# Second routed layer of a graph and mixture-of-experts network: how its experts' rows are weighted, fetched and summed

## The chip, the cores and the metric

The kernel runs on one core of a Trainium2 chip, as one program of 261270 instructions. The metric is the device time in microseconds (us); the time before is the median of three runs. A profiled execution, recorded by the hardware profiler, stands beside them with its own time and span. The engines are called PE (matrix multiplies, with PEld its weight loads), DVE, ACT and POOL (element work), SP (DMA issue); POOL and ACT issue DMAs too.

## The reference

Eight layers follow each other over 625 nodes of 512 features, each adding to x. The layer that the change touches is the fourth, a mixture of experts in two levels: 4 groups of 8 experts, of which each node takes 2 groups and in each group 2 experts.

```python
def _L1_ffn_ref(inp, ln_g, ln_b, wg_group, wg_inner, W1, b1, W2, b2, gln_g, gln_b):
    x = inp.reshape(-1, d)
    gw = _topk_gate(x @ wg_group, GK, G)              # GK = EK = 2, G = 4, E = 8
    z = _layernorm(x, ln_g, ln_b)
    out = jnp.zeros_like(x)
    for g in range(G):
        iw = _topk_gate(z @ wg_inner[g], EK, E)
        moe = jnp.zeros_like(z)
        for e in range(E):
            h = jax.nn.relu(z @ W1[g, e] + b1[g, e])
            moe = moe + iw[:, e:e + 1] * (h @ W2[g, e] + b2[g, e])
        y = _layernorm(z + moe, gln_g[g], gln_b[g])
        out = out + gw[:, g:g + 1] * y
    return out.reshape(b, t, d) + inp
```

The layer before it is a graph convolution (L1_gnn), the one behind it a routed graph convolution (L2_gnn), and behind that comes a recurrent layer (L2_ffn) which fills most of the span.

## The kernel before

The 625 nodes lie as five tiles (t = 0 to 4) of P = 125 rows. The kernel is written layer by layer; when it is built, a scheduler puts the instructions of each engine into one fixed order and sets the semaphores, so neighbouring layers and stages may mix. `tc.issue_after(i)` makes what its block issues on i's engine stand behind i in that order.

L1_ffn in stages. **Front**: the small weights (wg, wi, ln_g, ln_b, rb, gb) are loaded from ACT's queue (L1105, L1108, L106 in row_bcast, L1143 to L1145); x, normed, becomes xin (L153), z is its layer norm (L174, L175) and is written to the DRAM table `nodes`; both are transposed (L183) and copied by ACT (L186). **Routing**: gate logits on PE (L285), the best two per group, and from them, for each of the 4 choices (c) of a node, its expert, its rank within the expert (`rk`) and its score. `at` (L1219) is a one-hot matrix of ranks, `named` (L1207) one of experts weighted with the node's number; their product pw (L1220) summed gives `who`: which node sits in which of the 128 places (SLOTS) of each of the 32 experts (ALL). `to` gives, for each choice of each node, the row of the DRAM table `made` in which its result will be. A branch (L1276) calls L1_late where more than 128 nodes chose one expert; in these data it is not taken.

**Experts**: fetch(e) gathers an expert's 128 rows from `nodes` on POOL (L1154), ten experts ahead. places (transposes, L1307, copy xg L1310), first (eight PE passes, L1320, and a relu on ACT to hid, L1322) and second (one PE product y, L1328, an ACT copy ys, L1330, a 256 KB write to `made` from SP, L1331) run for experts 0 to 31. In iterations 2 to 16 inputs() puts in, one at a time, what doesn't depend on the experts: for each tile the bias sums (L1297, added to z by L1298 into zb[0] and zb[1], one for each of a node's two groups, j) and x + xin (POOL, L1293) with the gain's bias (L1292, L1294).

**Sum and norm**: take(j) gathers from `made` on POOL (L1340), two rows for each node and tile, into buffers r0 and r1, which j = 0 and j = 1 share. norm(j, ts) adds them to zb[j] times their scores (DVE, L1351), takes statistics (L1352, L1353), the root through ACT (L127 in rsqrt, with DVE's L128 to L132), and applies gain and weight (L1362 on PE, L1363, L1364 on DVE) to x. take(0) stands behind expert 24's work, as every j = 0 choice lies in groups 0 to 2; take(1) behind the last expert. C.seen takes the statistics of the finished x (L144 to L146), from which L2_gnn norms it (L153); that layer loads its adjacency counts m_count (L222, from SP), casts them (L191, L193), multiplies the gate (L285) and the counts (L237) and begins its expert products (L292).

Of the kernel before, what the change touches and what calls it, by code (L numbers as in the profile page):

```python
# [30 lines left out]
KC = D // 128  # L31
# [687 lines left out]
def L0_ffn(C):  # L719
# [11 lines left out]
    with ExitStack() as st:  # L731
# [24 lines left out]
        with ExitStack() as st2:  # L756
# [32 lines left out]

            C.made1 = C.dram.tile([4 * N + 32 * SLOTS, D], F32, name="made1")  # L790
            for r in range(0, 4 * N, 128):
                n = min(128, 4 * N - r)
                nc.sync.dma_start(C.made1[r:r + n], zero[:n])
# [244 lines left out]
def L1_gnn(C):  # L1038

    nc, tc, I = C.nc, C.tc, C.ins  # L1040
    with ExitStack() as st:
        E = st.enter_context
        pool = E(tc.tile_pool(name="b", bufs=1))
        ps = E(tc.tile_pool(name="b_ps", bufs=2, space=PSUM))
        bias = C.row_bcast(pool, I["L1_gnn_b"], D, "bias")
        m = C.load_graph(pool, "weighted")
        xn = pool.tile([P, NT, D], F32, name="xn")
        C.normed(xn)
        xT = pool.tile([128, KC, N], F32, name="xT")
        C.feature_major(ps, xT, xn)  # L1050
        w = C.w_next
        h = pool.tile([P, NT, D], F32, name="h")
        for t in range(NT):
            ph = ps.tile([P, D], F32, name="ph")
            C.linear(ph, xT, t, w)
            C.copy(t, h[:, t], ph)
        for t in range(NT):
            po = ps.tile([P, D], F32, name="ph")
            C.aggregate(po, m, t, h)
            y = pool.tile([P, D], F32, name="y", bufs=2)  # L1060
            nc.vector.tensor_add(y, po, bias[:P])
            nc.vector.scalar_tensor_tensor(y, y, 0.0, xn[:, t], op0=ALU.max, op1=ALU.add)
            nc.vector.tensor_add(C.x[:, t], C.x[:, t], y)
            C.seen(t)
    C.ahead.close()


def L1_ffn(C):
# [11 lines left out]
    with ExitStack() as st:  # L1080
# [20 lines left out]

        DENSE = G * N
        made = C.made1
        wg = pool.tile([128, KC, G], F32, name="wg")
        nc.scalar.dma_start(wg, W("wg_group").rearrange("(k p) g -> p k g", p=128))  # L1105
        wi = pool.tile([128, KC, G, EX], F32, name="wi")
        for g in range(G):
            nc.scalar.dma_start(wi[:, :, g], W("wg_inner")[g].rearrange("(k p) e -> p k e", p=128))  # L1108

        C.gate_w = C.small.tile([128, KC, 4], F32, name="gate_w", bufs=1)  # L1110
# [3 lines left out]
        z = pool.tile([P, NT, D], F32, name="z")  # L1114
        C.layernorm(z, xin, C.row_bcast(pool, W("ln_g"), D, "ln_g"), C.row_bcast(pool, W("ln_b"), D, "ln_b"))
        C.by_parts(nodes.rearrange("(t p) d -> p t d", p=P), z)
# [21 lines left out]

        rb, gb = R([128, D], "rb"), R([128, D], "gb")
        nc.gpsimd.memset(rb, 0.0)  # L1140
        nc.gpsimd.memset(gb, 0.0)
        for j in range(2):
            nc.scalar.dma_start(rb[32 * j:32 * j + 32], W("b2").rearrange("g e d -> (g e) d"))  # L1143
            nc.scalar.dma_start(rb[64 + 32 * j:64 + 32 * j + G], W("gln_g"))
        nc.scalar.dma_start(gb[64 + G:64 + 2 * G], W("gln_b"))  # L1145
        who_f, who = R([SLOTS, ALL], "who_f"), pool.tile([SLOTS, ALL], U32, name="who")
# [5 lines left out]
        def fetch(e):  # L1152
            fetched[e] = at_pool.tile([SLOTS, D], F32, name="at_e")
            nc.gpsimd.indirect_dma_start(out=fetched[e], out_offset=None, in_=nodes[:, :],  # L1154
                                         in_offset=bass.IndirectOffsetOnAxis(ap=who[:, e:e + 1], axis=0))

        with tc.tile_pool(name="c_ps", bufs=2, space=PSUM) as ps, tc.tile_pool(name="c_x", bufs=1) as xpool:
# [66 lines left out]
            for e in range(AT):  # L1224
                fetch(e)
            top = R([1, 1], "top")
# [17 lines left out]
            for i in range(2):  # L1244
                pick(score[:, 2 * i:2 * i + 2], ss_g[:, :, :G, i])
            pick(wj, gate[:, :, :G])
            nc.vector.tensor_tensor(tmp, OH, score[:, :, :, None].to_broadcast(wide4), ALU.mult)
# [17 lines left out]
            nc.vector.tensor_mul(beyond, beyond, lj)  # L1265
            nc.vector.tensor_add(slot[:, :2], slot[:, :2], beyond)
            nc.vector.tensor_mul(late[:, 2:], slot[:, 2:], lj)
            nc.vector.tensor_sub(slot[:, 2:], slot[:, 2:], late[:, 2:])
            nc.vector.tensor_copy(to, slot)
            nc.vector.tensor_tensor(score[:, :2], score[:, :2], lj, ALU.max)  # L1270
            nc.vector.tensor_mul(late[:, 2:], score[:, 2:], lj)
            nc.vector.tensor_sub(score[:, 2:], score[:, 2:], late[:, 2:])

# [50 lines left out]
        def second(e):  # L1324
# [4 lines left out]
            ys = work.tile([128, D], F32, name="ys", bufs=4)  # L1329
            nc.scalar.copy(ys[:SLOTS], y[:SLOTS])  # L1330
            nc.sync.dma_start(made[DENSE + e * SLOTS:DENSE + (e + 1) * SLOTS], ys[:SLOTS])  # L1331

        rows = {}

        def take(j):
            rows[j] = [work.tile([P, NT, D], F32, name=f"r{i}", bufs=1) for i in range(2)]
            upto = DENSE + (ALL - EX * (1 - j)) * SLOTS
            for t in range(NT):
                for i in range(2):
                    nc.gpsimd.indirect_dma_start(out=rows[j][i][:, t], out_offset=None, in_=made[:upto, :],  # L1340
                                                 in_offset=bass.IndirectOffsetOnAxis(ap=to[:, 2 * i + j, t:t + 1], axis=0))

        def norm(j, ts):
# [5 lines left out]
            for t in ts:  # L1349
                for i in range(2):  # L1350
                    nc.vector.scalar_tensor_tensor(moe[:, t], rows[j][i][:, t], score[:, 2 * i + j, t:t + 1], moe[:, t], op0=ALU.mult, op1=ALU.add)  # L1351
                nc.vector.bn_stats(st_[:, t], moe[:, t])  # L1352
                nc.vector.bn_aggr(mv[:, t], st_[:, t])  # L1353
# [13 lines left out]
        for e in range(ALL + 1):  # L1367
# [4 lines left out]
            if e:  # L1372
                second(e - 1)
            if 2 <= e < 17:
# [1025 lines left out]
```

## Time and profile before

| what | us |
|---|---|
| median of 3 runs (lowest, highest) | 4655.87 (4653.85, 4656.43) |
| the profiled execution | 4661.62 |
| its span (mean granted clock of PE 0.960) | 4659.8 |
| L1_ffn, from its first load to the last x (L1364) | 749.8 to 944.9 |
| `who` ready | 796.8 |
| first expert's transposes | 805.7 |
| take(0)'s ten issues | 886.0 to 900.7 |
| take(1)'s ten issues | 910.8 to 926.7 |
| first L292 of the next layer | 977.65 |

The engines' busy time in stretches of the layer (x counts instructions; PEclk is the granted clock of PE, 1 being full speed; DMA share is that of the 16 DMA engines; the last column is GB/s):

```profile
core 0: us, PE busy (x) PEld busy (x) DVE busy (x) ACT busy (x) POOL busy (x), PEclk, DMA share, GB/s
753.00:763.00 10.00, 0.02 (x1) 0.03 (x1) 8.47 (x23) 0.86 (x3) 5.74 (x5) 0.50 1.02 276
763.00:774.00 11.00, 11.00 (x83) 10.53 (x83) 7.25 (x37) 6.20 (x10) 0.00 (x0) 0.81 1.03 369
...
815.00:895.00 80.00, 80.00 (x434) 53.50 (x433) 24.16 (x36) 32.41 (x66) 25.12 (x25) 1.00 0.87 298
895.00:903.00 8.00, 0.93 (x9) 0.73 (x7) 4.91 (x11) 0.33 (x2) 4.77 (x4) 0.83 0.79 231
903.00:912.00 9.00, 8.10 (x12) 2.41 (x12) 8.50 (x27) 2.41 (x7) 1.19 (x1) 0.69 0.29 109
912.00:963.00 51.00, 24.42 (x74) 15.86 (x75) 37.49 (x113) 7.69 (x17) 11.97 (x10) 0.50 0.33 88
```

A row is read from left to right: in 815 to 895 PE is busy all 80 us at full clock; in 895 to 903 it has 0.93 us of work.

### The profile page before, as it was taken

To read this page: it belongs to the slowest core of one execution; us is meant where nothing else is said; L and a number is where in the kernel's file an instruction comes from. 1 tells how busy PE (TensorE), PEld (TensorE's weight loads), DVE (VectorE), ACT (ScalarE), POOL (GpSimd) and SP (SyncE) were. 2 spreads that over 40 slices of the span, in tenths; PEclk is the share of its full clock that TensorE was granted. 3 is DMA by queue.
4 is the path that set the end of the run, shared out by engine and by line. 5 is a ranking of instruction groups with operands and counts; after the bars stand their busy time and mean duration, and the time that the engine had idled before them with its cause. 6 is when DMAs were issued, how large, how long until landed. Compare 5 with 4: busy or idle time off the path is not lost. (4 is left out here: it accounts for less than half of the span.)

```text
span 4659.8 us, 261270 instructions
## 1 busy us (share of the span) xinstructions
PE 4305.1 (92%) x110568; PEld 3367.1 (72%) x110568; DVE 2735.3 (59%) x13565; ACT 1373.1 (29%) x5465; POOL 275.6 (6%) x777
## 2 busy tenths in 40 slices
PE   8998997889999799999999999999999999998888
PEld 6666764566566678888888888887888888887555
DVE  7535016431166566677667677766676777676358
ACT  8533111311156222222222222222222222222146
POOL 0000001300000000000000000000000000000001
PEclk9997997889999899999999999999999999999888
DMA  1131983711166222222222222221000000000200
GB/s 43 43 140 37 323 281 102 250 49 50 63 215 237 59 42 45 44 47 49 43 47 49 44 52 49 45 45 39 8 8 8 7 7 9 7 9 10 87 10 12
DMA packets 487820, 315.92 MB, mean 68 GB/s; under 512 B 287531, under 2 KB 386599, under 8 KB 486461
## 3 DMA queue, kind: packets, MB, share of 16 engines
q1 hardware_dynamic: 469706, 289.62, 22.5%
q0 software_dynamic: 8800, 16.92, 1.3%
q10 hardware_dynamic: 9092, 6.87, 0.6%
q8 instruction: 84, 1.38, 0.1%
q14 instruction: 138, 1.13, 0.1%
HBM read 261.52 MB, written 51.77 MB: 67 GB/s over the span
## 5 line engine op out<-in xcount | busy, mean ns | idle before, releaser
L2015 PE MATMUL pa<-wp,left 128*23 128x256 bf16 x32080 | 1011.2, 274 | 0.0
L2015 PEld LDWEIGHTS pa<-wp,left 128*23 128x23 bf16 x32080 | 816.3, 94 | 65.8 <-issue 4.4
L2015 PE MATMUL pb<-wp,left 128*23 128x128 bf16 x30000 | 541.3, 220 | 0.6
L2015 PEld LDWEIGHTS pb<-wp,left 128*23 128x23 bf16 x30000 | 491.5, 94 | 7.0 <-issue 2.5
L2103 ACT ACTIVATE seq<-ga 128x8 f32<-128x8 f32 x625 | 131.7, 211 | 1179.1 <-DVE ga L2161 1179.1
L2159 DVE STREAM_TRANSPOSE col<-pa 128x256 f32<-128x256 f32 x625 | 281.6, 451 | 303.7 <-PE pa L2015 303.4
L2003 PEld LDWEIGHTS pb<-wsel,cs 128*4 128x4 f32 x5000 | 151.0, 83 | 262.1 <-DVE cs L2170 241.0
L2073 PE MATMUL acc<-xslot,wslot 128*128 128x160 f32 x1250 | 337.7, 352 | 0.0
L2003 PE MATMUL pb<-wsel,cs 128*4 128x8 f32 x5000 | 217.1, 169 | 112.2 <-DVE cs L2170 45.3
L2030 PE MATMUL po<-o,left 128*23 128x128 f32 x5416 | 285.7, 281 | 13.4 <-issue 12.5
L2027 PE MATMUL po<-w,left 128*23 128x128 bf16 x14912 | 293.3, 219 | 0.0
L1991 POOL TENSOR_TENSOR seq<-seq,cs 128x4 f32<-128x4 f32 x625 | 126.3, 202 | 2648.7 <-ACT seq L2103 2648.7
L2096 ACT COPY xrow<-xlb 1x4 f32<-1x4 f32 x625 | 122.5, 196 | 540.4 <-ACTq L2094 540.4
L2153 DVE COPY col<-gxb 128x16 f32 x625 | 114.3, 183 | 219.0 <-issue 219.0
L2008 PE MATMUL pb<-wsel,left 128*4 128x8 f32 x5000 | 217.6, 170 | 25.6
L2073 PEld LDWEIGHTS acc<-xslot,wslot 128*128 128x128 f32 x1250 | 186.6, 189 | 67.7 <-issue 0.2
L2027 PEld LDWEIGHTS po<-w,left 128*23 128x23 bf16 x14912 | 234.7, 94 | 0.0
L2027 PE MATMUL po<-o_rest,left 128*23 128x128 bf16 x7588 | 220.5, 220 | 1.9 <-DMA o_rest<-parts_o 1.9
L2008 PEld LDWEIGHTS pb<-wsel,left 128*4 128x4 f32 x5000 | 150.3, 83 | 84.4 <-DVE left L2134 71.7
L2134 DVE TENSOR_TENSOR left<-th,so 128x4 f32<-128x4 f32 x625 | 104.2, 167 | 179.4 <-ACT so L2109 179.4
L2163 DVE STREAM_TRANSPOSE col<-pb 128x128 f32<-128x128 f32 x625 | 197.9, 317 | 6.0 <-PE pb L2015 4.8
L2168 DVE STREAM_TRANSPOSE col<-po 128x128 f32<-128x128 f32 x625 | 198.4, 317 | 2.8 <-PE po L2027 2.8
(555 smaller groups left out, 7119.2 us busy)
## 6 DMA issues: line engine op xcount, KB each, us to landing
ring<-in_L_ffn_W_dram SPq DMA_DIRECT2D x80, 1024.0 KB
xslot<-xTd SPq DMA_DIRECT2D x384, 80.0 KB
wslot<-in_L_ffn_WihT_dram SPq DMA_DIRECT2D x384, 64.0 KB
gxb<-gx SPq DMA_DIRECT2D x124, 160.0 KB
w<-in_L_ffn_WihT_dram SPq DMA_DIRECT2D x16, 1024.0 KB
raw<-in_L_ffn_WhhT_dram SPq DMA_DIRECT2D x28, 512.0 KB
made<-ys SPq DMA_DIRECT2D x39, 256.0 KB
w<-in_L_gnn_Wl_dram SPq DMA_DIRECT2D x8, 1024.0 KB
```

The source lines that it names most:

```text
L1991: pool.tensor_tensor(seq[:, 2, 1::2], seq[:, 1, 1::2], cell_c, ALU.mult).then_inc(sem["ifg"])
L2003: pe.matmul(lg, cs[:, 2 * s + 1:2 * s + 2].to_broadcast([128, S]), wsel[:, 1, s], start=s == 0, stop=False)
L2008: m = pe.matmul(lg, hT[:, s:s + 1].to_broadcast([128, S]), wsel[:, 0, s], start=False, stop=s == KC - 1)
L2015: m = pe.matmul(out[32 * j:32 * j + 2 * GAP + 1], upper[:, s, wide], wp[e][:, s, i, j, gs[0]:gs[1]].rearrange("p g n -> p (g n)"), start=k ...
L2027: m = pe.matmul(to, upper[:, s, wide], of(e, 3 * s - 3 + i)[:, j], start=False, stop=s == 3 and i == 2, skip_group_check=True)
L2030: m = pe.matmul(to.rearrange("p (u r) -> p u r", r=32), left[:, 0, :2 * GAP + 1], o0[e].rearrange("p (u j r) -> p j u r", u=4, j=4)[:, j], ...
L2073: pe.matmul(later, wslot, xslot, start=False, stop=True, skip_group_check=True).then_inc(used)
L2096: act.copy(xrow[:, :S], xlb[b % DEEP][:, :, u + 1]).then_inc(sem["x"])
L2103: act.activation(seq[:, 0:2, 1::2], ga[:, :8].rearrange("p (g s) -> p g s", g=2), AF.Sigmoid).then_inc(sem["if"])
L2159: dve.transpose(col[:, :8, :32], pa.rearrange("p (b r) -> p b r", r=32)).then_inc(sem["ta"])
L2163: dve.transpose(col[:, 8:12, :32], pb.rearrange("p (b r) -> p b r", r=32)).then_inc(sem["tb"])
L2168: dve.transpose(col[:, 12:, :32], po.rearrange("p (s r) -> p s r", r=32)).then_inc(sem["to"])
```

## The change

Four things in L1_ffn, with the first one's loads put into L1_gnn. Early: the twelve small loads move from ACT's queue to SP's, into a new function L1_early that L1_gnn calls behind its first transposes, with the two fills of rb and gb. Weighted rows: a second one-hot product, pws, of `at` with the scores (split into three bfloat16 parts that sum to the score) gives `scale`, the score of the node in each place of each expert; the copy of y out of PSUM multiplies by it. Gathers that add: take(j) gathers straight into zb[j] with an addition in the DMA; r0, r1 and the multiply-adds go, and a pair that is late (no place in its expert) points its second choice to a row of zeros, ZERO, by which `made` grows by one row. The gathers are written in a mixed order of tiles. Order: the POOL additions x + xin stand behind the first ten fetches, and all of norm(0), its roots on ACT among it, behind the last copy of y.

```diff
--- before.py
+++ after.py
@@ L0_ffn
-            C.made1 = C.dram.tile([4 * N + 32 * SLOTS, D], F32, name="made1")
+            C.made1 = C.dram.tile([4 * N + 1 + 32 * SLOTS, D], F32, name="made1")
...
@@ L1_gnn
         C.feature_major(ps, xT, xn)
         w = C.w_next
+        L1_early(C)
...
+def L1_early(C):
+
+    nc, G, EX = C.nc, 4, 8
+    W = lambda name: C.ins["L1_ffn_" + name]
+    C.early = C.stack.enter_context(ExitStack())
+    pool = C.early.enter_context(C.tc.tile_pool(name="c_early", bufs=1, side="right"))
+    wg, wi = (pool.tile([128, KC, *n], F32, name=k) for k, n in (("wg", (G,)), ("wi", (G, EX))))
+    ln = [pool.tile([128, D], F32, name=k) for k in ("ln_g", "ln_b")]
+    rb, gb = (pool.tile([128, D], F32, name=k) for k in ("rb", "gb"))
+    nc.gpsimd.memset(rb, 0.0)
+    nc.gpsimd.memset(gb, 0.0)
+    for t, k in zip(ln, ("ln_g", "ln_b")):
+        src = W(k)
+        nc.sync.dma_start(t, bass.AP(tensor=src.tensor, offset=src.offset, ap=[[0, 128], [1, D]]))
+    nc.sync.dma_start(wg, W("wg_group").rearrange("(k p) g -> p k g", p=128))
+    for g in range(G):
+        nc.sync.dma_start(wi[:, :, g], W("wg_inner")[g].rearrange("(k p) e -> p k e", p=128))
+    for j in range(2):
+        nc.sync.dma_start(rb[32 * j:32 * j + 32], W("b2").rearrange("g e d -> (g e) d"))
+        nc.sync.dma_start(rb[64 + 32 * j:64 + 32 * j + G], W("gln_g"))
+    nc.sync.dma_start(gb[64 + G:64 + 2 * G], W("gln_b"))
+    C.begun = wg, wi, ln, rb, gb
+
+
 def L1_ffn(C):
 
 
@@ -1099,20 +1124,15 @@
 
         nodes = C.dram.tile([N, D], F32, name="nodes1")
 
-        DENSE = G * N
+        ZERO, DENSE = G * N, G * N + 1
         made = C.made1
-        wg = pool.tile([128, KC, G], F32, name="wg")
-        nc.scalar.dma_start(wg, W("wg_group").rearrange("(k p) g -> p k g", p=128))
-        wi = pool.tile([128, KC, G, EX], F32, name="wi")
-        for g in range(G):
-            nc.scalar.dma_start(wi[:, :, g], W("wg_inner")[g].rearrange("(k p) e -> p k e", p=128))
-
+        wg, wi, ln, rb, gb = C.begun
         C.gate_w = C.small.tile([128, KC, 4], F32, name="gate_w", bufs=1)
         nc.scalar.dma_start(C.gate_w, I["L2_gnn_gate_W"].rearrange("(k p) e -> p k e", p=128))
         xin = pool.tile([P, NT, D], F32, name="xin")
         C.normed(xin)
         z = pool.tile([P, NT, D], F32, name="z")
-        C.layernorm(z, xin, C.row_bcast(pool, W("ln_g"), D, "ln_g"), C.row_bcast(pool, W("ln_b"), D, "ln_b"))
+        C.layernorm(z, xin, *ln)
         C.by_parts(nodes.rearrange("(t p) d -> p t d", p=P), z)
         load(RING)
         zT = pool.tile([128, KC, N], F32, name="zT")
@@ -1136,13 +1156,7 @@
         nc.vector.tensor_scalar(before, C.iota[:P, :P], part[:P], None, op0=ALU.is_gt)
         gT = pool.tile([128, N], F32, name="gT")
 
-        rb, gb = R([128, D], "rb"), R([128, D], "gb")
-        nc.gpsimd.memset(rb, 0.0)
-        nc.gpsimd.memset(gb, 0.0)
-        for j in range(2):
-            nc.scalar.dma_start(rb[32 * j:32 * j + 32], W("b2").rearrange("g e d -> (g e) d"))
-            nc.scalar.dma_start(rb[64 + 32 * j:64 + 32 * j + G], W("gln_g"))
-        nc.scalar.dma_start(gb[64 + G:64 + 2 * G], W("gln_b"))
+        scale = R([SLOTS, ALL], "scale")
         who_f, who = R([SLOTS, ALL], "who_f"), pool.tile([SLOTS, ALL], U32, name="who")
         to = pool.tile([P, 4, NT], U32, name="to")
         most = pool.tile([1, 1], I32, name="most")
@@ -1151,7 +1165,7 @@
 
         def fetch(e):
             fetched[e] = at_pool.tile([SLOTS, D], F32, name="at_e")
-            nc.gpsimd.indirect_dma_start(out=fetched[e], out_offset=None, in_=nodes[:, :],
+            return nc.gpsimd.indirect_dma_start(out=fetched[e], out_offset=None, in_=nodes[:, :],
                                          in_offset=bass.IndirectOffsetOnAxis(ap=who[:, e:e + 1], axis=0))
 
         with tc.tile_pool(name="c_ps", bufs=2, space=PSUM) as ps, tc.tile_pool(name="c_x", bufs=1) as xpool:
@@ -1222,7 +1236,7 @@
             nc.vector.reduce_sum(who_f, pw.rearrange("s h e -> s e h"), axis=AX.X)
             nc.vector.tensor_copy(who, who_f)
             for e in range(AT):
-                fetch(e)
+                last_fetch = fetch(e).ins
             top = R([1, 1], "top")
             nc.vector.tensor_add(base[0:1, 0], base[0:1, NT - 1], pn[0:1, 1, NT - 1])
             nc.vector.reduce_max(top, base[0:1, 0], axis=AX.X)
@@ -1243,6 +1257,20 @@
             nc.vector.tensor_add(gate, gate, second_)
             for i in range(2):
                 pick(score[:, 2 * i:2 * i + 2], ss_g[:, :, :G, i])
+            split, left = R1([P, 4, NT], "split"), [xpool.tile([P, 4, NT], BF16, name=f"score{h}") for h in range(3)]
+            scored = xpool.tile([P, 4, NT, 3, ALL], BF16, name="scored")
+            nc.vector.tensor_copy(left[0], score)
+            nc.vector.tensor_sub(split, score, left[0])
+            nc.vector.tensor_copy(left[1], split)
+            nc.vector.tensor_sub(left[2], split, left[1])
+            for h in range(3):
+                nc.vector.tensor_tensor(scored[:, :, :, h], OH, left[h][:, :, :, None].to_broadcast(wide4), ALU.mult)
+            pws = ps.tile([SLOTS, 3, ALL], F32, name="pws", bufs=1)
+            for c in range(4):
+                for t in range(NT):
+                    nc.tensor.matmul(pws.rearrange("s h e -> s (h e)"), at[:, c, t], scored[:, c, t].rearrange("p h e -> p (h e)"),
+                                     start=(c, t) == (0, 0), stop=(c, t) == (3, NT - 1))
+            nc.vector.reduce_sum(scale, pws.rearrange("s h e -> s e h"), axis=AX.X)
             pick(wj, gate[:, :, :G])
             nc.vector.tensor_tensor(tmp, OH, score[:, :, :, None].to_broadcast(wide4), ALU.mult)
             for j in range(2):
@@ -1264,12 +1292,11 @@
             nc.vector.tensor_sub(beyond, beyond, slot[:, :2])
             nc.vector.tensor_mul(beyond, beyond, lj)
             nc.vector.tensor_add(slot[:, :2], slot[:, :2], beyond)
+            nc.vector.tensor_scalar_add(slot[:, 2:], slot[:, 2:], -float(ZERO))
             nc.vector.tensor_mul(late[:, 2:], slot[:, 2:], lj)
             nc.vector.tensor_sub(slot[:, 2:], slot[:, 2:], late[:, 2:])
+            nc.vector.tensor_scalar_add(slot[:, 2:], slot[:, 2:], float(ZERO))
             nc.vector.tensor_copy(to, slot)
-            nc.vector.tensor_tensor(score[:, :2], score[:, :2], lj, ALU.max)
-            nc.vector.tensor_mul(late[:, 2:], score[:, 2:], lj)
-            nc.vector.tensor_sub(score[:, 2:], score[:, 2:], late[:, 2:])
 
 
         count = nc.values_load(most, min_val=0, max_val=N, skip_runtime_bounds_check_because="a number of nodes")
@@ -1290,7 +1317,8 @@
             po = ps_g.tile([P, D], F32, name="pg")
             if what == 2:
                 nc.tensor.matmul(po, gT[64:64 + 2 * G, cols], gb[64:64 + 2 * G], start=True, stop=True)
-                nc.gpsimd.tensor_add(C.x[:, t], C.x[:, t], xin[:, t])
+                with tc.issue_after(last_fetch):
+                    nc.gpsimd.tensor_add(C.x[:, t], C.x[:, t], xin[:, t])
                 nc.vector.tensor_add(C.x[:, t], C.x[:, t], po)
             else:
                 j = what
@@ -1327,18 +1355,16 @@
             y = ps_y.tile([128, D], F32, name="y")
             nc.tensor.matmul(y[:SLOTS], state.pop(e), loaded[g, ex // 4, "W2"][:, ex % 4], start=True, stop=True)
             ys = work.tile([128, D], F32, name="ys", bufs=4)
-            nc.scalar.copy(ys[:SLOTS], y[:SLOTS])
+            out = nc.scalar.activation(ys[:SLOTS], y[:SLOTS], AF.Copy, scale=scale[:, e:e + 1]).ins
             nc.sync.dma_start(made[DENSE + e * SLOTS:DENSE + (e + 1) * SLOTS], ys[:SLOTS])
-
-        rows = {}
+            return out
 
         def take(j):
-            rows[j] = [work.tile([P, NT, D], F32, name=f"r{i}", bufs=1) for i in range(2)]
             upto = DENSE + (ALL - EX * (1 - j)) * SLOTS
-            for t in range(NT):
-                for i in range(2):
-                    nc.gpsimd.indirect_dma_start(out=rows[j][i][:, t], out_offset=None, in_=made[:upto, :],
-                                                 in_offset=bass.IndirectOffsetOnAxis(ap=to[:, 2 * i + j, t:t + 1], axis=0))
+            for t, i in ((0, 0), (1, 0), (2, 0), (0, 1), (3, 0), (1, 1), (4, 0), (2, 1), (3, 1), (4, 1)):
+                nc.gpsimd.indirect_dma_start(out=zb[j][:, t], out_offset=None, in_=made[:upto, :],
+                                             in_offset=bass.IndirectOffsetOnAxis(ap=to[:, 2 * i + j, t:t + 1], axis=0),
+                                             compute_op=ALU.add)
 
         def norm(j, ts):
 
@@ -1347,8 +1373,6 @@
             mv = C.small.tile([P, NT, 2], F32, name="ln_mv")
             moe = zb[j]
             for t in ts:
-                for i in range(2):
-                    nc.vector.scalar_tensor_tensor(moe[:, t], rows[j][i][:, t], score[:, 2 * i + j, t:t + 1], moe[:, t], op0=ALU.mult, op1=ALU.add)
                 nc.vector.bn_stats(st_[:, t], moe[:, t])
                 nc.vector.bn_aggr(mv[:, t], st_[:, t])
             v = C.small.tile([P, NT], F32, name="ln_v")
@@ -1370,17 +1394,19 @@
             if e < ALL:
                 first(e)
             if e:
-                second(e - 1)
+                last_ys = second(e - 1)
             if 2 <= e < 17:
                 inputs(e - 2)
             if e == ALL - EX + 1:
                 take(0)
         take(1)
-        norm(0, (0, 1))
-        norm(0, (2, 3, 4))
+        with tc.issue_after(last_ys):
+            norm(0, (0, 1))
+            norm(0, (2, 3, 4))
         for ts in ((0, 1), (2, 3), (4,)):
             norm(1, ts)
             C.seen(*ts)
+    C.early.close()
 
 
 def L1_late(C, zT, tf, ss, b1, made):
```

More of the change, by code (lines that the diff above doesn't have):

```diff
@@ L788, in L0_ffn @@
                 nc.sync.dma_start(made[r:r + n], zero[:n])
-            C.made1 = C.dram.tile([4 * N + 32 * SLOTS, D], F32, name="made1")
-            for r in range(0, 4 * N, 128):
-                n = min(128, 4 * N - r)
+            C.made1 = C.dram.tile([4 * N + 1 + 32 * SLOTS, D], F32, name="made1")
+            for r in range(0, 4 * N + 1, 128):
+                n = min(128, 4 * N + 1 - r)
                 nc.sync.dma_start(C.made1[r:r + n], zero[:n])
```

## The prediction, made before the changed kernel was run

> **What bounds the kernel now.** I read the cores first: one core, span 4659.8 us, in a profiled run of 4661.62 us; the median shown is 4655.87 us. The sum below is made against the profiled span and its gain taken off the median, so the 5.75 us between them drop out. I take 0.2%, 9.3 us, as about what a measurement of this kernel can tell from no change.
>
> Most of the span is the recurrent layer behind (the costliest lines of the groups are L2015, L2027, L2073); its instruction order is unchanged, so I carry it over as a constant. The diff lives in 750 to 978 us. There I read the waits, then the timeline where the longest end.
>
> ```profile
> core 0: 4659.8 us, clock 0.960
> ```
>
> The waits of 745 to 950 us (engine, its line, what it waited for: total, times, longest):
>
> ```profile
> POOL at_e L1154 <- DVE who L1223: 37.6, 1, 37.6
> ACT rs_s L127 <- DVE ln_v L1355: 26.4, 3, 17.8
> ...
> DVE zb L1351 <- DMA r<-made,to: 20.0, 4, 16.4
> ...
> PE pt L183 <- ACT xT L186: 10.1, 1, 10.1
> ...
> POOL r L1340 <- DVE zb L1363: 10.1, 1, 10.1
> ...
> PE y L1328 <- ACT hid L1322: 7.5, 1, 7.5
> ```
>
> The timeline at the end of the experts (start, duration, engine, line):
>
> ```profile
> 892.85 0.59 ACT L1330 COPY ys<-y 128x512 f32<-128x512 f32 x1 [0.49 <-PE y L1328]
> ...
> 893.98 1.28 ACT L127 ACT_TABLE_LOAD   x1
> ...
> 902.93 0.20 ACT L127 ACTIVATE rs_s<-ln_v 125x2 f32<-125x2 f32 x1 [7.67 <-DVE ln_v L1355]
> 903.04 0.35 ACT L1322 ACTIVATE hid<-ph,b 128x128 f32<-128x128 f32 x1
> ...
> 903.44 3.76 PE L1328 MATMUL y<-ring,hid 128*128 128x512 f32 x4 [7.51 <-ACT hid L1322]
> ...
> 907.24 0.59 ACT L1330 COPY ys<-y 128x512 f32<-128x512 f32 x1 [1.10 <-PE y L1328]
> ...
> 910.81 1.46 POOL L1340 DMA_INDIRECT r<-made,to  x1 [10.10 <-DVE zb L1363]
> ```
>
> ACT stands in its root for DVE's first statistics from 894 to 902.93, and the last experts' hid stands behind it: PE sits idle 7.51 us. Then ys31 at 907.24, its row write, and only at 910.81 the second ten gathers. DVE's last wait on them ends at 929.27, the last x is:
>
> ```profile
> 944.19 0.75 DVE L1364 SCALAR_TENSOR_TENSOR x<-z,ln_r,x 125x512 f32<-125x512 f32 x1
> ```
>
> I call its end A0 = 944.94. From A0 the next layer needs 32.7 us to its first L292 (977.65). Of the gathers themselves:
>
> ```profile
> L1340 POOL DMA_INDIRECT r<-made,to x20: 1180/1196/1530, 886.0 to 925.2; - x20
> ...
> DMA to landing us min/median/max: 5.3/5.8/8.0
> ```
>
> **The change, part by part.**
>
> *Small loads.* ACT issues twelve of them from 749.84 to 761.22 and copies the first xT only at 762.35; PE waits 10.1 us for that. Gone, ACT is free by 751, but DVE still produces the xin tiles until 758 and had its z start held only 1.53 us (for ln_g, 760.43). The five POOL additions at 752.2 to 759.5 leave too; under them DVE's xin took up to 1.08 instead of 0.53 us and single small operations 0.55 to 0.69 instead of about 0.15, together about 1.5 us. Sum: who comes about 3.0 us sooner (bounds -5 to +0.5, since PE's granted clock was 0.81 in 763 to 774 and 0.50 after, and an earlier start may see more of the slow one). The loads go to SP a layer sooner, ahead of the nodes load there. That load is issued at 421.54 and first read at 444.64, so the twelve issues (about 11 us by ACT's row) are covered; uncovered, they would cost those 11. Two POOL fills (0.52 and 0.80) stand near the attention's end, 0 to 1.3; I take 0.
>
> *Weights before the gather.* DVE gets three products like L1207 (0.78 each), a reduction (0.23) and some eight operations of 0.15 to 0.2; three go. PE gets 20 pairs like L1220 (3.3 us then, paced by DVE's 0.167 masks, which exist already). All but one copy stand behind who, where fetches run anyway; who to the first expert was 8.9 us, I take 10.4: +1.5 (bounds 0 to +3). The L1330 copy with a per-row factor stays a pass of 585 ns. The pointer row ZERO costs two small DVE additions where three score operations go, behind the branch; made's clearing keeps its number of stores.
>
> *Additions behind the fetches.* Two L1297 pairs that stood ahead of the branch move into the loop: an iteration with one took 3.48 us against 2.22, so two cost 2 x 1.26 = +2.5. The POOL additions now hold a few fetches by about 6.5 us, hidden by fetching ten experts (22 us) ahead; uncovered, that 6.5 is a stall of the experts.
>
> *Roots behind the experts.* Table load and roots stand behind ys31. Without the stall PE's last y in the present run would end near 898.0 and its copy at 898.8, against 907.24 + 0.59: 9 us. With -3.0, +1.5 and +2.5, y31 ends at 899.0. The stall's place is taken by another wait. In the built order SP's 112-row piece of m_count (1.37 MB), freed by the last y, stands ahead of the last made write. The present load ran about 946 to 953.5 at some 300 GB/s, so 4.6 us lie ahead; then the write and its completion, 2.9 us in this run (907.9 to 910.81). Second gathers start at T1 = 899.5 + 4.6 + 2.9 plus about 1 for the other gathers in flight = 908 (bounds 902.5, if the two transfers share the engines, to 911.5).
>
> *Gathers that add.* r and its ten plus ten L1351 (0.75 each, 14.8 us of DVE) go, and with them the wait of take(1) for r. The price is unknown: no DMA here adds. Near bound: a plain gather, issue 1.2 at a period of 1.5, landing 5.3. Far bound: two plain landings one after the other, 11.6, as if the destination were fetched first. It is nearest to the plain row, since the rows and bytes fetched are the same: I take 6.2. Each tile's second gather waits on POOL's queue for the landing of its first, and everything behind it in that queue waits too. The built order is tiles 0, 1, 2, 3, then 0 and 1 again, 4, 2, 3, 4. So with landing L the fifth issue is at start + max(6, L), the sixth 1.5 later. Take(0) starts at 887 and its last landing is near 908.6, norm(0) ends some 10 us later, 918.6. In take(1) tile 1 is whole at T1 + max(6, L) + 1.5 + L = 908 + 6.2 + 1.5 + 6.2 = 921.9. From there DVE has one tile's statistics, the root chain and four passes (5 to 6.5 us by the operations from 923.56 on), then the stretch that ran unbroken from 933.15 to 944.94: 11.8. Together 17.5. A0 = 939.4, a gain of 5.5.
>
> [...]
>
> *Next layer.* m_count is there before A0, so its casts no longer end the wait of the first pa product (962.63, A0 + 17.7). What stays is PE's own slow-clock work: transposes 4.7, gate products 8.5 and some pa. I take A0 to L292 as 30.7 instead of 32.7: gain 2 (bounds 0 to 6).
>
> Sum: 5.5 + 2 = 7.5, taken as 7: 4655.87 - 7 = **4649** us.
>
> **The rivals.**
>
> *Adding gathers are slow* (the other side). At L = 10 take(0) issues at 887, 897, 898.5, then 900, 901.5, 903 and the last at 910, so POOL is free only at 911.5; tile 1 of take(1) is whole at 911.5 + 10 + 1.5 + 10 = 933, A0 = 950.5, a loss of 5.6 less 2: about 4659.5. At L = 12 the same gives T1 = 915.5, tile 1 at 941, A0 = 958.5: a loss of 11.6 after the next layer's 2, 4667. It decides from L near 9; beyond that each us costs 4. For it: no such DMA was seen, and the longest plain landing is 8.0 already. Against: the DMA share of take(1)'s stretch leaves a third of the engines free.
>
> *Nothing is won.* m_count ahead of the last write gives T1 = 911.5 and L = 8 the rest: tile 1 at 929, A0 = 946.5, less 2: 4655.4. For it: the built order of SP. Against: both must come late together.
>
> *All of it is won.* The write shares the engines with m_count (T1 = 903, 5 sooner), A0 = 936 as norm(0) then ends only at 918.6 and DVE goes on from there with all tiles landed, and the next layer gains 6: 9 + 6 = 15, 4641. For it: the clock is 1.00 over 815 to 895, and PE kept busy to the end. Against: PE's granted clock at the transition is 0.50 whatever DVE does.
>
> *The early loads bring nothing*, as DVE's own chain to who holds: who 0 instead of 3 sooner moves y31 and T1 by 3: 4652, inside the forecast's own range.
>
> **How the numbers follow.** Forecast 0.52, own range 4643 to 4653 (T1 905 to 911, L 5.3 to 8); of it 0.20 lies beyond the 9.3 us. All won 0.22, nothing won 0.12, slow gathers 0.14, nearly all of it past +0.2%, since a price beyond the turning point climbs at 4 us for one. Faster 0.20 + 0.22 = 0.42, same 0.32 + 0.12 = 0.44, slower 0.14. The range for 8 in 10 reaches half into the full gain and to L = 11: 4636 to 4664.
>
> **What would show it.** In the trace after: ACT's first xT copy near 752 to 754, who about 3 us sooner; no 7.5 us idle of PE ahead of y; ys31 near 899; the first gather of the second ten near 908, waiting on made's last write, with m_count landing just ahead; landings of 6 to 7 us; no wait of POOL above 1 us within a ten; the last x near 939; L292 some 30.7 us after it. Landings over 9 us, or fetches late for the experts, make the prediction wrong upward; second gathers at 903 make it wrong downward.

## The result, and the profile after

The changed kernel is slower: 4679.68 us (4677.03 to 4681.09, five runs) against 4656.43 (4653.85 to 4661.01), a ratio of 1.0046 with a 95% interval of 1.0035 to 1.0058. The forecast was 4649, a gain of 7; it lost 23. The profiled execution took 4681.09, with a span of 4679.3.

The waits of the changed kernel between 745 and 1000 us (the columns as before), cut to those that answer to the ones shown of before:

```profile
DVE ln_st L1376 <- DMA zb<-made,to: 48.6, 5, 41.5
ACT rs_s L127 <- DVE ln_v L1379: 48.5, 4, 20.0
...
POOL zb L1365 <- DMA made<-ys: 15.5, 1, 15.5
...
POOL zb L1365 <- DMA zb<-made,to: 12.9, 4, 4.1
...
POOL z L1365 <- DMA z<-made,to: 8.9, 3, 5.5
```

PE's wait for ACT's hid has left the list, as forecast. In its place DVE stands 41.5 us for the first sum (before 16.4), and POOL waits for its own gathers, seven times. The gathers, by their line:

```profile
L1365 POOL DMA_INDIRECT zb<-made,to x10: 1972/1982/2027, 893.4 to 925.7; - x10
L1365 POOL DMA_INDIRECT z<-made,to x10: 1982/1983/2366, 928.0 to 956.9; - x10
```

An issue takes 1.98 us where a plain gather's took 1.20. The timeline at the place where the forecast had the second ten start (908):

```profile
893.42 2.03 POOL L1365 DMA_INDIRECT zb<-made,to  x1 [15.50 <-DMA made<-ys]
...
904.19 1.97 POOL L1365 DMA_INDIRECT zb<-made,to  x1 [1.85 <-DMA zb<-made,to]
905.27 3.19 SPq L222 DMA_DIRECT2D m_count<-graph_count  x1
908.57 2.03 SPq L1359 DMA_DIRECT2D made<-ys  x1
909.93 1.98 POOL L1365 DMA_INDIRECT zb<-made,to  x1 [3.76 <-DMA zb<-made,to]
...
920.60 1.98 POOL L1365 DMA_INDIRECT zb<-made,to  x1 [4.12 <-DMA zb<-made,to]
923.36 0.69 DVE L1376 BATCH_NORM_STATS2 ln_st<-zb 125x6 f32<-125x512 f32 x1 [41.47 <-DMA zb<-made,to]
...
928.02 2.00 POOL L1365 DMA_INDIRECT z<-made,to  x1 [0.30 <-issue]
```

The fifth gather adds to the tile of the first and is let go 10.8 us after the first was issued (904.19 - 893.42). Between 904 and 928 PE has almost nothing to do: the busy time by stretches (columns as in the table before the prediction) shows 1.45 us of PE in 24, where the kernel before has 15.46 in the same 24.

```profile
818.00:904.00 86.00, 86.00 (x449) 55.80 (x448) 23.72 (x35) 35.75 (x70) 31.71 (x28) 1.00 0.84 275
904.00:928.00 24.00, 1.45 (x4) 0.37 (x2) 2.23 (x6) 2.17 (x3) 11.87 (x6) 0.54 0.94 183
928.00:960.00 32.00, 12.15 (x14) 3.87 (x14) 18.18 (x49) 0.41 (x2) 20.52 (x10) 0.50 0.63 81
```

The last x ends at 971.92 (before 944.94) and the first L292 is at 1001.53 (before 977.65): 23.9 us later. Of these, 2.3 lie ahead of the layer, which starts later in this profile; the other 21.5 are lost in it.

### The profile page after: what moved, and what is told of

It reads as the page before. It is cut to its first block, busy times and chain, and to the rows that moved or that the text cites. A ratio compares the mean times of both kernels' runs of the same rounds, so it can differ in the third digit from the quotient of the medians.

```text
span 4679.3 us, 261292 instructions
## 1 busy us (share of the span) xinstructions
PE 4300.7 (92%) x110588; PEld 3362.3 (72%) x110588; DVE 2726.1 (58%) x13552; ACT 1376.1 (29%) x5465; POOL 292.1 (6%) x777
## 5 line engine op out<-in xcount | busy, mean ns | idle before, releaser
L2029 PEld LDWEIGHTS pb<-wsel,cs 128*4 128x4 f32 x5000 | 150.9, 83 | 265.7 <-DVE cs L2196 238.5
```

Source lines behind the costliest of these rows:

```text
L2029: pe.matmul(lg, cs[:, 2 * s + 1:2 * s + 2].to_broadcast([128, S]), wsel[:, 1, s], start=s == 0, stop=False)
```

## The experiments

The profiles start the layer up to 3 us apart, so the marks are counted from the end of the last x of L1_gnn in the same profile (L1063's last addition, 749.69 in the kernel before). "Last y" is the end of PE's last expert product, "second ten" the first issue of take(1), "L292" its first weight load. The ratio is to the kernel before on the same chip, with its 95% interval. From L292 to the end, where the kernels hardly differ, the profiles take 3674 to 3686 us, a spread that no run explains; so a part is priced by the marks, and the median, which carries that spread, stands beside them.

| kernel | first y | last y | second ten | last x | L292 | median | ratio |
|---|---|---|---|---|---|---|---|
| before | 64.3 | 157.5 | 161.1 | 195.3 | 228.0 | 4656.43 | 1 |
| changed | 65.5 | 151.5 | 176.0 | 219.9 | 249.5 | 4679.68 | 1.0046 [1.0035, 1.0058] |
| plain gathers | 65.4 | 151.2 | 167.9 | 203.5 | 231.1 | 4670.86 | 1.0039 [1.0026, 1.0053] |
| before + adding gathers | 72.5 | 191.8 | 196.1 | 237.3 | 266.3 | 4703.35 | 1.0109 [1.0093, 1.0126] |
| own accumulators | 72.3 | 157.2 | 181.1 | 226.6 | 256.3 | 4692.31 | 1.0084 [1.0070, 1.0098] |
| m_count behind last write | 64.8 | 150.9 | 176.9 | 219.6 | 249.4 | 4685.32 | 1.0065 [1.0051, 1.0079] |
| roots free | 65.4 | 182.6 | 192.1 | 232.3 | 262.5 | 4696.05 | 1.0089 [1.0076, 1.0102] |
| plain, m_count behind | 65.0 | 151.5 | 169.9 | 205.2 | 235.3 | 4673.60 | 1.0035 [1.0022, 1.0047] |
| before + roots order | 69.3 | 152.5 | 161.5 | 197.2 | 225.8 | 4655.62 | 0.9996 [0.9987, 1.0005] |
| before + early loads | 64.1 | 157.2 | 166.1 | 200.4 | 230.4 | 4661.78 | 1.0009 [0.9998, 1.0020] |
| changed, m_count away | 65.5 | 151.3 | 170.9 | 212.7 | 245.3 | 4681.94 | 1.0050 [1.0037, 1.0064] |
| plain, m_count away | 65.4 | 151.2 | 160.6 | 196.0 | 227.5 | 4666.93 | 1.0017 [1.0008, 1.0026] |
| early + roots + away | 69.1 | 152.4 | 161.9 | 197.5 | 228.3 | 4658.35 | 1.0001 [0.9992, 1.0010] |
| the same + POOL order | 62.4 | 146.0 | 156.1 | 191.8 | 222.1 | 4654.61 | 0.9994 [0.9985, 1.0003] |
| own accumulators, away | 65.5 | 152.3 | 171.1 | 217.0 | 248.2 | 4684.17 | 1.0045 [1.0030, 1.0061] |
| the best + own rows | 63.2 | 146.4 | 155.8 | 192.7 | 224.2 | 4654.51 | 0.9983 [0.9970, 0.9995] |

**Plain gathers.** The rows go to r0 and r1 again, and DVE adds them:

```diff
-   indirect_dma_start(out=zb[j][:, t], ..., compute_op=ALU.add)
+   indirect_dma_start(out=rows[j][i][:, t], ...)
...
+   for i in range(2):
+       nc.vector.tensor_add(moe[:, t], moe[:, t], rows[j][i][:, t])
```

> The changed kernel with plain gathers again: rows go into r0 and r1 as before, and DVE adds them to zb (ten tensor additions for each group instead of an addition in the DMA); early loads, weighted rows and both orders stay. Theory A, the adding gathers cost the time (a period of 2.29 us against 1.50, landings of 9 to 20 us against 5.8, and the second gather of a tile waiting for the first): the second ten gathers start near 908 to 912 us instead of 928, the last x ends near 944, and the time is about 4653 us (4646 to 4660). Theory B, the other edits cost it (m_count's load ahead of the last row write, the first ten starting at 893 instead of 886, the slower weighted copy): the time stays above 4668.

4670.86: the time is the one that theory B named, and the ratios of the two kernels (1.0039 and 1.0046) lie within each other's intervals. Yet by the marks 18 of the 21.5 us at L292 came back, as theory A has it; behind L292 this profile takes 3685.9 us and that of the changed kernel 3677.8, so the medians hide most of it. The second ten still started only at 167.9. The timeline names what stood there:

```profile
901.98 1.20 POOL L1369 DMA_INDIRECT r<-made,to  x1 [0.31 <-issue]
...
903.18 0.33 SPq L222 DMA_DIRECT2D m_count<-graph_count  x1
...
905.46 1.40 POOL L1369 DMA_INDIRECT r<-made,to  x1 [0.31 <-issue]
...
917.28 0.69 DVE L1380 TENSOR_TENSOR zb<-zb,r 125x512 f32<-125x512 f32 x1 [8.38 <-DMA r<-made,to]
...
919.19 1.19 POOL L1369 DMA_INDIRECT r<-made,to  x1 [12.33 <-DVE zb L1380]
```

Three of the first ten, the eighth issued at 901.98 and the last at 905.46, are under way beside m_count's load. The eighth is summed only at 917.28, 15.3 us after its issue, and the ninth and tenth right behind it; the second ten need the buffers.

**Before, with the weighted rows and adding gathers alone** (early loads and both orders undone in the changed kernel).

> The kernel before with the weighted rows and the adding gathers alone: small loads on ACT's queue in the layer itself, the POOL additions and the roots of norm(0) where the scheduler puts them. Theory A: the second ten start near 922 to 928, and the time is about 4677 (4668 to 4688). Theory B: 4656 within 6.

4703.35, above even theory A's range. With the roots where the scheduler puts them, ACT stands in the first one until the late sums come, so the last y ends at 191.8; and the front was 8 us slower (first y 72.5) at a granted clock of PE of 0.50, of which more below.

**Own accumulators.** Each tile's second gather adds into a cleared buffer `apart`, so no gather waits for another.

```diff
+   apart = [work.tile([P, NT, D], F32, name=f"apart{j}", bufs=1) for j in range(2)]
+   nc.vector.memset(apart[j], 0.0)
...
-   out=zb[j][:, t]
+   out=(zb[j], apart[j])[i][:, t]
```

> The changed kernel with the second gather of each tile adding into a buffer of its own, cleared beforehand, which DVE then adds to zb (five more DVE additions for each group): all twenty gathers still add, but none waits for another's landing. Theory A1, the serial waits are the larger part: issues follow each other at 2.29 us, the first ten end 23 us after their start instead of 34, the second likewise, and the time falls to about 4665 (4660 to 4670). Theory A2, the transfers themselves are the limit (the DMA engines take twice as long for each adding row): the issues come sooner, the landings stay as late, and the time is above 4672.

4692.31, but unclear: clearing on DVE held the first experts (first y 72.3), and m_count's load, issued from 910.77 to 919.65, lay over the first ten gathers, issued from 898.62 to 921.25.

**m_count behind the last row write**, in the changed kernel (`tc.issue_after` of the last made write around the load).

> The changed kernel with the load of m_count ordered behind the last made write on SP's queue. Theory A: the second ten wait for POOL to finish the first ten, at 928 whatever SP does, so no change, 4680 within 4. Theory B, m_count ahead of the last write holds the second ten: 5 us less, 4675 or below.

4685.32, second ten at 176.9 beside 176.0: no gain, theory A, a little above its range.

**Roots free**: the changed kernel without the order around norm(0).

> The changed kernel without the order that puts norm(0)'s roots behind the last copy of y. Theory A, the first sums are late because the gathers add: ACT stands in the root from about 894 us until DVE's first statistics at 923, the last experts' hid stand behind it, and the last row write and the second ten gathers come near 932 to 940: 4686 to 4694 us, slower than the changed kernel. Rival, the order is worth nothing since POOL holds the second ten until 928 anyway: 4676 to 4684.

4696.05, theory A, a little above its range: the order is needed once the sums are late; the last y moved from 151.5 to 182.6.

**Plain gathers, m_count behind the last write.**

> The changed kernel with plain gathers (as in the run with plain gathers) and m_count's load ordered behind the last made write. Theory D, in the run with plain gathers the 1.37 MB load, started at 903 in the middle of the first ten gathers, held their last landing until 917, and with it the buffers r for the second ten (919): behind the last write it starts a little later and no longer holds that write, so the second ten start near 911 and the time falls by 6 to 9 us, to about 4663 (4658 to 4667). Rival, the two transfers share the DMA engines in either order: 4668 to 4673.

4673.60, second ten at 169.9: the rival, at the top of its range. The order of the two transfers on SP does not matter here: second ten at 169.9 with the load behind the write, at 167.9 with it ahead.

**Before with the roots order alone.**

```diff
+   with tc.issue_after(last_ys):
        norm(0, (0, 1))
        norm(0, (2, 3, 4))
```

> The kernel before with one edit alone: norm(0)'s roots and table load behind the last copy of ys. Theory E, the 7.5 us for which PE stood at the last experts go, and m_count keeps its old place behind everything: the last y ends near 898, the second ten gathers start when the buffers r are free (about 905), the time falls by 5 to 8 us, 4645 to 4651 beside 4653 to 4656. Rival, the stall only covered what waits anyway (the landing of the first ten, buffers r): within 2 us of before.

0.9996: no change that can be told, so the rival held. In the profile the last y comes 83.2 us after the first instead of about 93, yet the second ten start 9.0 us after the last y where it was 3.6.

**Before with the early loads alone.**

> The kernel before with the early loads alone. Theory D: the early pool changes where the next layer's buffers lie, so that m_count's load waits for the last y alone and stands ahead of the last made write; the front gains about 1.5 us, the second ten gathers lose 3 to 6, the next layer gains 2 to 3: within 4 us of before. Rival, the early loads are a plain gain: 4 us or more faster than before.

1.0009, as theory D: first y unchanged (64.1 beside 64.3), m_count's load at 907.69 ahead of the last row write, the second ten 5.0 us later.

**m_count kept away**, first in the changed kernel, then with plain gathers:

```diff
-   count = C.load_graph(first, "count")
+   with tc.issue_after(C.behind):        # the root of norm(1) for tiles 2, 3
+       for a, b in ((0, 112), (112, P)):
+           nc.scalar.dma_start(count[a:b], C.graph["count"][a:b])
```

> The changed kernel with m_count loaded from ACT's queue behind the root of norm(1) for tiles 2 and 3, so that no 1.37 MB load runs beside the gathers. Theory A, the adding gathers alone hold the end: their landings of 10 to 12 us and the 2.29 us period stay, the second ten start at 922 to 928, and at most 6 us are won: 4672 to 4680. Rival, the load held the adding gathers as it held the plain ones: 4664 to 4670.

> The same with plain gathers (DVE adds). Theory D', whichever of the two transfers stands first on SP's queue, the load shares the DMA engines with the last of the first ten gathers, in packets of 12.5 KB, and holds their landing until 917: kept away, the first ten land by 911, the second ten start at 911 to 913 instead of 919, and the time is about 4664 (4659 to 4668). Rival, something else costs the plain version its 15 us: 4669 to 4674.

The pair prices the adding gathers with nothing beside them. Adding: second ten at 170.9, last x 212.7, L292 245.3, 4681.94. Plain: 160.6, 196.0, 227.5, 4666.93. The adding version is a little above theory A's range. The fronts are alike (first y 65.5 and 65.4, last y 151.3 and 151.2). The difference is 17.8 us at L292 and 15.0 in the medians. The waits of the two, from 880 us on, adding first:

```profile
DVE ln_st L1376 <- DMA zb<-made,to: 43.8, 5, 33.7
...
POOL zb L1365 <- DMA zb<-made,to: 8.9, 3, 4.3
POOL z L1365 <- DMA z<-made,to: 7.8, 3, 5.1
```

```profile
DVE zb L1380 <- DMA r<-made,to: 22.1, 6, 16.7
...
POOL r L1369 <- DMA made<-ys: 14.4, 1, 14.4
...
POOL r L1369 <- DVE zb L1380: 5.1, 1, 5.1
```

In the plain one POOL waits for no gather, only once for DVE to have read the buffers r. Its 4666.93 lies in the range of theory D', and 9 above before on the same chip (4657.55): something else costs too.

**The order and the early loads without weighted rows**, and then with the POOL additions behind the fetches:

> The kernel before with the early loads and the roots behind the experts, m_count kept away in the same manner; no weighted rows, no adding gathers, POOL additions where the scheduler puts them. By the marks of the two single runs: first y 64 us after the layer's start, 83 us of loop, second ten at 157, last x near 192: 4649 (4644 to 4654), faster than before. If the weighted rows are not what else costs time, it is no faster than the plain version above.

> As the run before, and the POOL additions behind the first ten fetches. The additions no longer stretch DVE in the front (about 1.5 us won to who), but two bias products move into the loop (2.5 us lost): within 3 us of the run before. If the additions behind the fetches are what costs the changed kernel its loop, 4 us or more slower.

4658.35 missed its range; the second, 4654.61, is 3.7 less, just outside its own, and was the fastest till then, though not clear of no change. Against the plain version with m_count away it differs by the weighted rows alone: first y 62.4 beside 65.4, the loop (first to last y) 83.6 beside 85.8, L292 222.1 beside 227.5. So the weighted rows cost 5.4 us at L292. The medians differ by 12.3; the rest arises behind L292 (3686.1 and 3674.4 us in the two profiles), and why isn't shown.

**Own accumulators, m_count away, cleared on POOL** (the earlier experiment without its two disturbances).

> The changed kernel with m_count kept away (ACT's queue, behind norm(1)) and the second gather of each tile adding into a buffer of its own, cleared by POOL during the experts: all twenty add, none waits for another. Beside the run with m_count kept away alone, whose second ten start at 922 and whose last x is at 963. Theory A1, the serial waits are a good part of the price: the first ten end 23 us after their start (914 instead of 922), the second ten likewise, last x at 955 or before, 5 to 10 us faster, 4672 to 4677. Theory A2, issue and landing are the price: last x no sooner than 961, 4678 to 4684.

A2, just above its range: 4684.17, last x at 969.2. The second ten issue without a wait, 23.4 us from the start of the first to the end of the last (29.9 with the waits), but start no sooner (171.1 beside 170.9), and the last x comes later (217.0 beside 212.7). For what they stand until 923.33 the profile names nothing; the last row write, whose packets run beside the adding gathers until 921.4, is the likely reason.

**The best with rows of its own for the second ten** (xin, zT and one tile).

> The version without weighted rows and adding gathers, with the early loads, both orders and m_count kept away, and buffers of their own for the second ten gathers (xin, whose last reader is long done, zT and one more tile), so that they no longer wait for DVE to have read the first ten. Theory F, the shared buffers r hold the second ten from the last row write (about 901 by the marks of that version, 898.1 + 2.9) to 907.6: last x 5 to 6 us sooner, 4649 (4645 to 4652), clearly faster than before. Rival, the first ten's DVE work (norm(0)) ends only at about 916 and DVE has the same work behind it: last x at most 2 us sooner, 4652 to 4657.

Theory F fell and the time is the rival's, though this is the only version clear of no change on the right side: 0.9983. Over the version before it (0.9994) no gain is shown; the two intervals overlap. The second ten start at 155.8 where that version had 156.1, and now the wait is named:

```profile
907.65 1.34 POOL L1361 DMA_INDIRECT xin<-made,to  x1 [4.96 <-DMA made<-ys]
```

It is the last row write, put out on SP at about 899 and landed by 907.65: 8.7 us, where the kernel before took 2.9 at most, after its first ten had landed. In those 8.7 us the gathers' queue holds 53.0% of the 16 engines' time and SP's 21.8%; in the 2.9 us of before no other queue moved anything. So the removed stall comes back as a slower write beside the first ten gathers.

## Why the prediction was wrong

**The step that failed** is the bound of an adding gather: "issue 1.2 at a period of 1.5" was used at both ends, and landing was taken as 6.2, "nearest to the plain row, since the rows and bytes fetched are the same". Measured were an issue of 1.98 at a period of 2.29, and landings, read off the six waits of POOL in the run with m_count away (from the issue of a tile's first gather to that of its second), of 9.8 to 13.2 us; in the changed kernel itself, beside m_count, of up to 20.2. So even the far bound of 11.6 was passed, and that POOL's own time could grow was not bounded at all. The reason given for the choice was wrong in a way that the queue's line shows. In the pair with m_count away, from 890 to 972 us, plain first (packets, MB, share of the 16 engines' time):

```profile
q0 software_dynamic: 4480, 5.14, 24.2%
```

```profile
q0 software_dynamic: 8320, 5.17, 48.1%
```

The bytes are the same, the packets are not: 3840 more for 20 gathers, 192 each, and the engines are busy with them twice as long. In the trace of before the plain gathers' rows go mostly in packets of 4096 bytes, two rows at a time (1200 of them, beside 100 of one row), with a median of 159 ns each; in that of the changed kernel the adding gathers' go in packets of 2048, one row (2500 of them), with a median of 178 ns. With 23 us instead of 15 to issue ten, and landings about twice as long, take(0)'s issues lasted from 893.4 to 927.7 (34 us; the forecast had 21, the last landing included), and T1 came at 928 instead of 908.

**The rival "adding gathers are slow"** named the right mechanism at the right place. Its own price was low: at L = 10 to 12 it gave 4659.5 to 4667. Missing were the longer issue, and the first ten starting 5.1 us later in the layer than before; the plain versions with and without weighted rows, m_count away, differ there by 5.0 (140.2, 135.2).

**The serial waits**, which the forecast and the rival made the core of the price, are not it. With accumulators of their own the waits vanish and nothing is won; the last x comes at 217.0 where it came at 212.7, and the engines' time for the packets stays (46.6% over the same stretch). So the waits are not what makes the change slow.

**The free engines** were misread. The prediction held a third of the engines, free in take(1)'s stretch, against slow gathers; the row of before is that of 916 to 921, with a DMA share of 0.66:

```profile
916.00:921.00 5.00, 1.00 (x2) 0.00 (x0) 3.41 (x5) 0.00 (x0) 4.08 (x4) 0.50 0.66 172
```

But several gathers were in flight there, issued 1.5 us apart and landing after 5.8. Where one gather is alone the share is 0.32 of 16 engines for the last plain one of before and 0.34 for the last adding one of the run with m_count away, the time of about five engines each:

```profile
929.20:930.20 1.00, 0.00 (x0) 0.00 (x0) 0.93 (x3) 0.00 (x0) 0.00 (x0) 0.50 0.32 133
```

```profile
954.00:956.50 2.50, 0.89 (x1) 0.49 (x2) 2.46 (x11) 0.41 (x2) 0.00 (x0) 0.50 0.34 59
```

About the same share of the engines moved 133 GB/s for the plain gather and 59 for the adding one. So the free third of the engines was of no use to a single one.

**Small loads.** Right that PE's 10.1 us wait for ACT's xT goes; that it is worth 3 us of who isn't shown. Alone, the early loads leave the first y where it was (64.1, 64.3), which speaks for the rival "the early loads bring nothing"; but in that profile PE's granted clock from 13.3 to 28.3 us of the layer was 0.61, in the one of before 0.73. In the changed kernel, at 0.61 too, `who` comes at 45.7, 1.4 sooner than before.

**POOL additions.** Put at 1.5 us within the front; putting them behind the fetches took 6.7 off the first y (69.1 to 62.4). Some 1.9 of it is there at the first z (9.4 after the layer's start, then 7.5); the rest arises where PE's granted clock differs (0.50 and 0.61 from 13.3 to 28.3 us), below. But the two pairs that move into the loop were put down to this edit; the version with it and without weighted rows keeps them ahead of the branch, and the version with the weighted rows and without it doesn't, so it is the weighted rows that push them.

**Weighted rows.** Forecast +1.5 to the first expert and +2.5 in the loop; the pair of kernels gives +3.0 and +2.2. So 5.2 in place of 4.0, of which 3.0 was to be covered by the sooner who. The copy with a factor takes 687 ns, not the 585 that I kept.

**Roots.** The stall went as forecast: last y at 151.5 where the stall had it at 157.5. What did not come is the second ten's share. With plain gathers they wait for the shared buffers r, and with rows of their own for the write, whose landing takes 8.7 us instead of the 2.9 that the sum carried over from a quiet moment.

**m_count.** That its load starts early was right, and so is its cost in the plain version (231.1 beside 227.5 at L292); the early loads bring it about, since the single run with them shows it and the run with the roots alone (load at 949.98) does not; that it is by their pool is argued, not shown. The forecast put the price on SP's order, as 4.6 us from a load at some 300 GB/s. From 946 to 953.5 the kernel before moved 210, and the second ten of the plain version lose 7.3 (167.9 beside 160.6). The run with the order turned round, and a DMA share of 0.96 from 903 to 917.3 in the plain version, show that it is the shared engines.

**The next layer.** Last x to L292 is 29.6 (forecast 30.7, before 32.7): right in size. That m_count's early load is the reason isn't shown: the version with the roots alone has 28.6 with the load after the last x.

By the marks at L292 the sum reads: early loads, both orders, m_count away -5.9 (222.1); weighted rows +5.4 (227.5); adding gathers +17.8 (245.3); m_count's early load +4.2 (249.5): 21.5 later than before. The first term compares profiles with different clocks in the front, and the last doesn't show in the medians (1.0046 with the early load, 1.0050 without).

## What to carry to other kernels

An operation that no trace has shown is bounded in each of its times, the issuing engine's too (1.98 us here, where the forecast had 1.2), and the far end is taken until a row speaks for the near one; "the same bytes" said little here, where 5.14 MB went in 4480 packets and 5.17 MB in 8320. How many engines one transfer uses is read where it is alone (0.32 of 16 for a plain gather), not from the share of a stretch with several in flight (0.66). The last row write's time in a quiet moment, 2.9 us, didn't hold once an edit moved it beside the gathers, where it took 8.7: when a stall is removed, the price of the next step is looked up where it will then stand. The early loads, most likely by their buffer pool, let a later layer's load start early (907.69 with them alone, where before had 945.41), into the middle of the transfers that set the end.

## What the runs showed of the hardware

PE's granted clock differed between two executions of the same instructions, 0.73 and 0.50 in the same stretch, and `who` came 5.9 us later in the second. The front of the kernel before and of the version with the roots order alone has the same instructions in the same order. Before, then the roots version, whose layer starts 2.6 us later, in the same two stretches of the layer (columns as above):

```profile
763.00:778.00 15.00, 15.00 (x102) 14.53 (x102) 8.28 (x47) 6.20 (x10) 0.00 (x0) 0.73 0.95 340
778.00:785.00 7.00, 2.62 (x13) 2.49 (x12) 5.02 (x64) 0.23 (x1) 0.00 (x0) 0.50 0.03 10
```

```profile
765.62:780.62 15.00, 15.00 (x74) 14.49 (x72) 6.46 (x31) 6.02 (x10) 0.00 (x0) 0.50 0.92 336
780.62:787.62 7.00, 7.00 (x35) 7.00 (x35) 1.78 (x19) 0.00 (x0) 0.00 (x0) 0.50 0.01 4
```

PE is busy throughout the first stretch in both, at a PEclk of 0.73 and of 0.50, and does 102 instructions or 74 in it: `who` comes 47.1 us after the layer's start in one and 53.0 in the other. The kernel before ran between 4648 and 4669 us over all jobs, the quickest with a mean granted clock of 0.962 to 0.964, the longest with 0.958 to 0.961. So differences of some us between single profiles are read from the marks of a stage, and those that lie in the front, with the clock beside them.

The 1.37 MB load, in packets of 12.5 KB, held the small gathers that shared the engines with it: the eighth of the first ten took 15.3 us from issue to sum beside it, 8.0 in the run with the load away (901.77 to 909.75).

A gather of 125 rows of 2 KB, alone, took the time of about 5 of the 16 engines (a share of 0.32, plain; 0.34, adding) and moved 133 GB/s, or 59 when it added.
